# Two-layer binary convolution and local attention: new priorities and costs in a list planner, and the first image's channel sums on VectorE

## The chip, the cores and the metric

The kernel runs on one core of a Trainium2 chip. The metric is device time in microseconds (us) of one launch. The engines are TensorE (PE in the profile; PEld are its weight loads), VectorE (DVE), ScalarE (ACT), GpSimd (POOL) and SyncE (SP), which here only issues DMAs.

## The reference, cut to what matters

The input x has 16 images of 256 channels, 56 x 56 pixels, float32. Two layers follow each other, each a residual addition of a function of the group-normalized input (`_gn`: 32 groups of 8 channels).

```python
# layer 0
xq = sign(_gn(x) + bias)
for i, d in enumerate((1, 3, 5)):            # dilations
    wq = scale_i * sign(w[i] - mean(w[i]))   # binary weights, forward value
    y = conv3x3(xq, wq, dilation=d, groups=4) + cb[i] - move1[i]
    y = where(y >= 0, y, alpha[i] * y) + move2[i]
    out = out + y
out = (out - mean(out, channels)) * rsqrt(var(out, channels) + eps)
x = x + out * gamma + beta
# layer 1
q, k, v = split(_gn(x) @ qkv_w.T + qkv_b)     # 8 heads of 8 channels
k, v = branch(k) + rpb, branch(v)             # 9 neighbours, plus a learned 3x3 depthwise conv
attn = softmax over the 9 neighbours of sum_c(q * k)
x = x + (sum_9(attn * v) @ proj_w.T + proj_b)
```

The 3 x 3 neighbourhood of a pixel is the window of keys and values for that pixel.

## The kernel before, in words

An image is cut by halves of its rows: 128 partitions hold 64 channels of one group (there are NG = 4 groups g) for two half images. For the later steps a half is cut again into strips of 7 rows, so that one *unit* u (of NU = 2) covers 128 x 784 elements per group.

Per image b the steps are these, each with the name of its stage in the table `ORDER`:

- `signs`: loads the four groups as `xh` (three buffers), takes their sum and their sum of squares with two ACT passes (`stats`, L424: Identity and Square with an accumulated output), turns them into a shift per channel (`norm0`, lines L382 to L443) and writes the sign as bfloat16 into `sgn[g]` (stage "sign", L449), with two small DMAs for the rows at the border of the halves (`halo`). The first image has its own stage "start" that does all of it group by group from one load; later images load every group twice.
- `conv` ("conv0", "conv1" for the two units): per group and dilation 36 matmuls (L499) into one PSUM tile `ps` of two banks (there are four), then ACT and DVE steps (L518, L525, L531, L537) that add the parametric ReLU into `ct` (seven buffers). For one tile that is one ACT and two DVE steps, or two and one for the first dilation.
- `channel_norm` ("mean", "var", "root", "scale" for each unit): sums over channels by matmul (L548, L566), the normalized result, and its addition to `xt` (three buffers, loaded from x in stage "load") on POOL (L638) with a square pass on ACT (L645).
- `fold` and `qkv`: group norm of the second layer is folded into the weights (L667 to L717); six groups of 32 matmuls (L729) and ACT evictions (L747) fill `qt`, `kt`, `vt`, of which there is one each.
- `scores` ("prod", "term", "soft"): nine products q * shifted k (L785, POOL), ten groups of matmuls over heads (L807), then a softmax with DVE transposes (L821 to L843).
- `attend` ("value", "proj"): ten groups of matmuls (L857), products with shifted v (L869, DVE), sums of these (L883, POOL), projection (L903), the last addition (L914) and the store.

Nothing of the order of these operations is written out by hand. The code that builds the kernel first collects every operation in a `Plan`, with engine, an assumed cost, what it reads and writes, which buffers it takes, and a priority: twice the image number plus a number from `ORDER` for its stage and index (lower goes first). `Plan.emit` then simulates all engines at build time: among the operations that are ready and have their buffers, each engine's candidate is the one that can start first; an operation of better priority is preferred if it starts at most `AHEAD` later. The engine whose candidate starts first emits it. Buffers of the kinds xh, xt, ct, p and m are handed out in the order of their creation. A result is seen by another engine `HOP` later. `either` marks operations that POOL or DVE may do; DVE is a candidate only if it would end more than `LEAN` before POOL (for the last image `LAST`, a negative number). A set `port` flag keeps such an operation apart from POOL's in the plan. On the chip the engines then run their queues in that order and wait on semaphores for what they read and write.

Three lines carry the rule:

```python
self.prio = 2 * b + ORDER[stage][i]
elif start + cost + o.lean > done: continue
if e not in best or start < best[e][0] - self.AHEAD: best[e] = (start, x, e, cost)
```

Of the kernel before, what the change touches and what calls it, by code (L numbers as in the profile page):

```python
# [68 lines left out]
class Op:  # L69
# [6 lines left out]

ORDER = {
    "first": (-3.81,),
    "second": (88.59,),
    "start": (-2.38, 18.89, -7.71, 3.29),  # L80
    "weights": (-4.65, -9.01, 0.64, 24.68, 23.33, 21),
    "stats": (10.49, 30.86, 22.58, 94.91),
    "norm0": (32.82,),
    "sign": (19.48, 99.46, -6.27, -5.4),
    "conv0": (-1.69, 4.96, 26.11, 0.66, 0.85, 19.36, -4.07, -1.86, 4.93, -11.22, -8.26, 19.59),
    "conv1": (-5.78, -8.78, 98.87, 0.22, 0.26, 6.89, -8.83, 30.63, 33.62, 1.84, 19.38, 25.39),
    "load0": (90.92,),
    "load1": (8.24,),
    "mean0": (-9.77,),
    "mean1": (20.13,),  # L90
    "var0": (-12.01, -8.88, 19.47, -0.22),
    "var1": (-14.66, 26.56, 89.22, -12.67),
    "root0": (23.78,),
    "root1": (-9.89,),
    "scale0": (100.7, 21.53, 3.58, 99.01),
    "scale1": (-10.73, -4.27, -0.4, 21.4),
    "fold": (-8.77,),
    "qkv0": (-0.15, -11.55, 19.01),
    "qkv1": (10.85, 1.84, 96.23),
    "prod0": (28.81, -0.84, -7.11, -6.13, -10.3, 7.62, -0.09, -4.95, 20.71),  # L100
    "prod1": (27.44, 23.38, -3.2, 99.25, 31.01, -10.92, -1.88, -1.61, -3.25),
    "term0": (19.37, 27.66, 25.15, 17.81, -9.38, 9.45, -1.68, 20.87, -1.36, 21.48),
    "term1": (24.14, 22.52, 28.6, 3.33, 8.91, 2.55, 1.92, 35.5, 4.7, 21.73),
    "soft0": (-4.91,),
    "soft1": (7.25,),
    "value0": (8.34, -0.46, -5.88, 1.95, 0.4, 8.91, 0.58, 26.08, -5.98, 34.72),
    "value1": (21.66, 7.27, 7.39, -4.86, -1.41, 9.39, 20.85, -1.49, -3.81, 90.17),
    "proj0": (0.69, 1.29, 9.01, -2.1),
    "proj1": (-14.76, 0.33, -4.01, -0.55),
# [3 lines left out]
class Plan:  # L113
# [7 lines left out]
    HOP = 0.1  # L121
    LEAN = 26.94
    LAST = -11.31
    AHEAD = 0.13

    def __init__(self, kinds):
        self.kinds, self.ops, self.wrote, self.read = kinds, [], {}, {}
        self.prio = 0.0
        self.queues = {k: [] for k in ("xh", "xt", "ct", "p", "m")}
# [106 lines left out]
def preact_conv_attention(  # L236
# [107 lines left out]
    def act(cost, f, r, w):  # L344
        op("ACT", 0.94 * cost, f, r, w)
# [887 lines left out]
```

## Time and profile before

| | |
|---|---|
| median of 3 runs | 2155.05 us (2154.48 to 2155.28) |
| the profiled execution's own time | 2157.43 us |
| its span, first to last instruction | 2154.9 us |
| mean granted TensorE clock | 0.948 |
| instructions | 70853 |
| DMA: read / written HBM | 154.91 MB / 51.38 MB, 96 GB/s over the span |

Busy time is the share of the span in which an engine has an instruction under way. Idle time is put down to what ended it, as far as semaphores show that. The chain of waits is followed backward from the last instruction: to what released each step, or to the step before it on its engine. Matmuls are pipelined, and their ends are modelled, so a busy PE isn't PE at its peak. "issue" is idle time for which the profile shows no releaser.

### The profile page before, as it was taken

How to read it: one execution, taken by the hardware profiler on the slowest of the kernel's cores; microseconds unless marked ns; L12 is line 12 of the kernel's file. 1: busy time of each engine (PE TensorE's matmuls, PEld its weight loads, DVE VectorE, ACT ScalarE, POOL GpSimd, SP SyncE). 2: the span in 40 equal slices, each digit the busy share in tenths (PEclk: the TensorE clock that was granted, in tenths of full speed). 3: DMA queues.
4: the chain of work that ended last, by engine and by line, in shares of the span. 5: the costliest groups of instructions: out<-in, count | busy, mean ns of one | idle time of the engine just before them, and what ended most of it. 6: DMA issues, size and time to landing. Idle time of an engine off the chain costs nothing.

```text
span 2154.9 us, 70853 instructions
## 1 busy us (share of the span) xinstructions
PE 1823.2 (85%) x31770; PEld 889.5 (41%) x31770; DVE 1697.7 (79%) x2327; ACT 1189.6 (55%) x1581; POOL 1276.5 (59%) x762
## 2 busy tenths in 40 slices
PE   6679898888989889898988989898898989879684
PEld 5444353434435343443534344353434435434231
DVE  7676969789696977969698796968879696986856
ACT  8675556565565756556575655647565565533220
POOL 2116657585675748557574865747486574746743
PEclk9889999999999999999999999999999999989896
DMA  8742534644453454445445444644444454041212
GB/s 208 165 92 67 123 79 111 130 95 91 110 130 83 111 121 97 93 104 133 91 111 117 100 94 95 138 94 111 108 102 101 95 133 100 7 100 23 61 31 60
DMA packets 102416, 216.26 MB, mean 100 GB/s; under 512 B 10720, under 2 KB 84832, under 8 KB 102112
## 3 DMA queue, kind: packets, MB, share of 16 engines
q1 hardware_dynamic: 102112, 211.74, 44.5%
q8 instruction: 248, 4.06, 0.8%
q14 instruction: 56, 0.46, 0.1%
HBM read 154.91 MB, written 51.38 MB: 96 GB/s over the span
## 4 chain that ended last, share of the span: by engine, by line
PE 42%; DVE 32%; POOL 10%; ACT 7%; issue 7%; DMA 2%; SPq 0%; POOLq 0%; DVEq 0%; ACTq 0%
PE banks L499 13%; PE banks L729 10%; PE banks L807 8%; POOL m L883 6%; DVE m L869 6%; DVE ct L537 6%; PE banks L857 5%; DVE ct L525 5%; DVE xt L914 4%; ACT banks L531 3%; DVE ct L595 3%; POOL xt L638 2%; PE banks L566 2%; PE banks L903 2%; DVE et L821 1%
## 5 line engine op out<-in xcount | busy, mean ns | idle before, releaser
L499 PE MATMUL banks<-sgn,wconv 64*64 64x392 bf16 x13824 | 680.2, 340 | 78.9 <-DVE m L869 32.1
L785 POOL TENSOR_TENSOR p<-qt,kt 128x784 f32<-128x784 f32 x276 | 467.0, 1726 | 326.2 <-ACT kt L762 179.3
L883 POOL TENSOR_TENSOR m<-m 128x784 f32<-128x784 f32 x251 | 478.3, 1906 | 248.1 <-DVE m L869 232.8
L499 PEld LDWEIGHTS <-wconv 64*64 64x64 bf16 x13824 | 438.6, 107 | 373.4 <-issue 217.4
L531 ACT ACTIVATE banks<-banks,cbi,csc 128x784 f32<-128x784 f32 x384 | 370.2, 973 | 203.2 <-DVE ct L525 192.4
L537 DVE SCALAR_TENSOR_TENSOR ct<-banks,oalpha,ct 128x784 f32<-128x784 f32 x384 | 389.4, 1027 | 98.4 <-ACT banks L531 89.3
L525 DVE SCALAR_TENSOR_TENSOR ct<-banks,asc,ct 128x784 f32<-128x784 f32 x256 | 262.0, 1024 | 186.9 <-PE banks L499 180.7
L857 PE MATMUL banks<-at,wv 64*32 64x392 f32 x5120 | 300.0, 533 | 61.3 <-DVE m L869 44.2
L638 POOL TENSOR_TENSOR xt<-xt,ct 128x784 f32<-128x784 f32 x128 | 237.2, 1860 | 190.4 <-DVE ct L624 189.6
L869 DVE TENSOR_TENSOR m<-banks,vt 128x784 f32<-128x784 f32 x288 | 278.2, 969 | 54.8 <-PE banks L857 48.7
L807 PE MATMUL banks<-p,wk 32*64 32x392 f32 x4608 | 245.4, 517 | 38.6 <-POOL p L785 38.2
L729 PE MATMUL banks<-xt,wf 64*64 64x392 f32 x3072 | 269.0, 496 | 2.8 <-POOL wf L667 2.8
L424 ACT ACTIVATE junk<-xh 128x1568 bf16<-128x1568 f32 x128 | 193.2, 1509 | 103.2 <-DMA xh<-in_x 101.4
L645 ACT ACTIVATE junk<-xt,pr 128x784 bf16<-128x784 f32 x128 | 121.2, 947 | 106.4 <-POOL xt L638 105.2
L602 ACT ACTIVATE sq<-ct 128x784 f32<-128x784 f32 x128 | 109.4, 857 | 125.2 <-DVE ct L595 102.5
L518 ACT ACTIVATE ct<-banks,asc 128x784 f32<-128x784 f32 x128 | 116.4, 910 | 98.8 <-PE banks L499 87.5
L729 PEld LDWEIGHTS banks<-xt,wf 64*64 64x64 f32 x3072 | 116.0, 134 | 129.2 <-issue 104.4
L857 PEld LDWEIGHTS banks<-at,wv 64*32 64x32 f32 x5120 | 63.3, 108 | 220.6 <-DVE m L869 110.9
L807 PEld LDWEIGHTS banks<-p,wk 32*64 32x64 f32 x4608 | 80.3, 133 | 161.1 <-POOL p L785 83.0
L903 PE MATMUL banks<-m,wp 64*64 64x392 f32 x1024 | 122.3, 584 | 26.1 <-DVE m L891 21.8
L595 DVE SCALAR_TENSOR_TENSOR ct<-ct,mv,banks 128x784 f32<-128x784 f32 x128 | 125.4, 1023 | 17.4 <-PE banks L566 17.4
L914 DVE SCALAR_TENSOR_TENSOR xt<-banks,prb,xt 128x784 f32<-128x784 f32 x128 | 128.1, 1028 | 10.4 <-PE banks L903 9.7
(102 smaller groups left out, 1518.8 us busy)
## 6 DMA issues: line engine op xcount, KB each, us to landing
xh<-in_x SPq DMA_DIRECT2D x248, 392.0 KB, 5.6
xt<-in_x SPq DMA_DIRECT2D x128, 392.0 KB, 7.1
out<-xt SPq DMA_DIRECT2D x128, 392.0 KB, 5.8
sgn<-sgn SPq DMA_DIRECT2D x128, 41.2 KB, 4.7
p<-in_w SPq DMA_DIRECT2D x12, 144.0 KB, 5.9
wq<-in_wqkv SPq DMA_DIRECT2D x1, 384.0 KB, 6.1
cst<-in_consts SPq DMA_DIRECT2D x1, 336.0 KB, 2.9
wk<-in_wk_a SPq DMA_DIRECT2D x1, 320.0 KB, 5.8
```

The source lines that it names most:

```text
L499: nc.tensor.matmul(out=ps[q * GC : (q + 1) * GC, h, 0:SN], lhsT=wconv[h * GC : (h + 1) * GC, g, d, tap, :], rhs=sgn[g][h * GC : (h + 1) * ...
L525: lambda: nc.vector.scalar_tensor_tensor(ct.tile, n(), asc[:, g, s], ct.tile, ALU.mult, ALU.add),
L531: lambda: nc.scalar.activation(n(), n(), AF.Relu, bias=cbi[:, g, s], scale=csc[:, g, s]),
L537: lambda: nc.vector.scalar_tensor_tensor(ct.tile, n(), oalpha[:, g, s], ct.tile, ALU.mult, ALU.add),
L638: lambda e, g=g: e.tensor_tensor(xt[:, g], xt[:, g], ct[g].tile, ALU.add),
L729: nc.tensor.matmul(out=ps[h * D : (h + 1) * D, q, 0:SN], lhsT=wf[q * GC : (q + 1) * GC, g, j, :], rhs=xt[q * GC : (q + 1) * GC, g, h, :], ...
L785: e.tensor_tensor(p.tile.rearrange("p x (r w) -> p x r w", w=W), _view(qt[:, 0, u * SN :], [(NU * SN + LANES, 2), (W, SR), (1, W)]), shift ...
L807: nc.tensor.matmul(out=ps[rt // 2][q * 64 : (q + 1) * 64, rt % 2, 0:n], lhsT=wk[r, j, :], rhs=rhs, start=s == 0, stop=s == 9,)
L857: nc.tensor.matmul(out=ps[rt * 32 : (rt + 1) * 32, q, 0:SN], lhsT=wv[q * 64 : (q + 1) * 64, j, :], rhs=at[q * 64 : (q + 1) * 64, rt, 0:SN] ...
L869: lambda j=j, m=m, ps=ps: nc.vector.tensor_tensor(m.tile.rearrange("p x (r w) -> p x r w", w=W), _view(ps[:, 0, :], [(512, 2), (W, SR), (1 ...
L883: lambda e, m=m, acc=acc: e.tensor_tensor(acc.tile, acc.tile, m.tile, ALU.add),
L914: lambda g=g, ps=ps: nc.vector.scalar_tensor_tensor(xt[:, g], ps[:, :, 0:SN], prb[:, g : g + 1], xt[:, g], ALU.add, ALU.add),
```

## The change

Every number in `ORDER` is replaced, as are the four constants of the plan. The table gets keys of their own for the first image (`^`) and the last (`$`); in this version their numbers equal those of the images between. Nearly all assumed costs are lowered, and the common factors 0.94 (ACT) and 0.965 (DVE) go. The first image's four Identity passes on ACT become four `tensor_reduce` on DVE; the Square passes stay. The diff, cut; of the three spellings of a new key the plain one is shown:

```diff
 ORDER = {
-    "first": (-3.81,),
-    "second": (88.59,),
-    "start": (-2.38, 18.89, -7.71, 3.29),
-    "weights": (-4.65, -9.01, 0.64, 24.68, 23.33, 21),
-    "stats": (10.49, 30.86, 22.58, 94.91),
-    "norm0": (32.82,),
-    "sign": (19.48, 99.46, -6.27, -5.4),
-    "conv0": (-1.69, 4.96, 26.11, 0.66, 0.85, 19.36, -4.07, -1.86, 4.93, -11.22, -8.26, 19.59),
-    "conv1": (-5.78, -8.78, 98.87, 0.22, 0.26, 6.89, -8.83, 30.63, 33.62, 1.84, 19.38, 25.39),
-    "load0": (90.92,),
-    "load1": (8.24,),
-    "mean0": (-9.77,),
-    "mean1": (20.13,),
-    "var0": (-12.01, -8.88, 19.47, -0.22),
-    "var1": (-14.66, 26.56, 89.22, -12.67),
-    "root0": (23.78,),
-    "root1": (-9.89,),
-    "scale0": (100.7, 21.53, 3.58, 99.01),
-    "scale1": (-10.73, -4.27, -0.4, 21.4),
-    "fold": (-8.77,),
-    "qkv0": (-0.15, -11.55, 19.01),
-    "qkv1": (10.85, 1.84, 96.23),
-    "prod0": (28.81, -0.84, -7.11, -6.13, -10.3, 7.62, -0.09, -4.95, 20.71),
-    "prod1": (27.44, 23.38, -3.2, 99.25, 31.01, -10.92, -1.88, -1.61, -3.25),
-    "term0": (19.37, 27.66, 25.15, 17.81, -9.38, 9.45, -1.68, 20.87, -1.36, 21.48),
-    "term1": (24.14, 22.52, 28.6, 3.33, 8.91, 2.55, 1.92, 35.5, 4.7, 21.73),
-    "soft0": (-4.91,),
-    "soft1": (7.25,),
-    "value0": (8.34, -0.46, -5.88, 1.95, 0.4, 8.91, 0.58, 26.08, -5.98, 34.72),
-    "value1": (21.66, 7.27, 7.39, -4.86, -1.41, 9.39, 20.85, -1.49, -3.81, 90.17),
-    "proj0": (0.69, 1.29, 9.01, -2.1),
-    "proj1": (-14.76, 0.33, -4.01, -0.55),
+    "first^": (24.59,),
+    "second^": (30.61,),
+    "start^": (-0.44, 12.01, 8.32, -11.9),
+    "weights^": (16.57, 0.74, 15.54, 8.13, -15.35, 9.81),
+    "stats": (-23.02, -11.03, 24.25, 43.57),
+    "norm0": (-20.32,),
+    "sign": (-8.81, 4.11, 13.27, 36.85),
+    "conv0": (-17.27, 2.29, 28.55, -15.99, 8.45, 8.78, -5.4, 6.78, 31.53, -11.69, 14.22, 14.25),
+    "conv1": (7.4, 12.95, 95.96, 12.79, 1.59, 12.9, 4.7, 39.18, 55.69, -8.93, 9.19, 30.54),
+    "load0": (95.98,),
+    "load1": (5.24,),
+    "mean0": (8.83,),
+    "mean1": (29.44,),
+    "var0": (8.78, 11.01, 15.97, 29.02),
+    "var1": (-9.01, 16.63, 18.58, 16.63),
+    "root0": (-10.53,),
+    "root1": (-17.05,),
+    "scale0": (15.67, 15.06, -3, 40.43),
+    "scale1": (-16.84, 17.23, 8.22, 8.83),
+    "fold": (-12.89,),
+    "qkv0": (6.66, -12.93, 15),
+    "qkv1": (8.11, -17.4, 96.15),
+    "prod0": (9.09, 30.51, 9.14, -13.48, 29.6, 14.43, 17.51, -16.64, -13.31),
+    "prod1": (-14.1, 12.39, 13.44, 5.73, 7.96, 13.89, -14.32, -16.31, -9.81),
+    "term0": (-17.28, 5.04, -6.13, -15.6, 8.43, 19.29, 31.53, 24.74, -8.75, 0.82),
+    "term1": (-16.84, 29.94, 29.34, 11.93, 6.96, 8.07, -9.43, 13.66, 9.05, 6.97),
+    "soft0": (-14.93,),
+    "soft1": (7.31,),
+    "value0": (-13.35, -23.05, -1.34, 4.34, -6.07, 9.15, -16.95, -21.09, -15.61, 39.19),
+    "value1": (-19.04, 4.84, -9.61, -12.73, 6.92, 7.45, 12.47, 8.08, 28.72, 39.07),
+    "proj0": (-0.81, 7.32, -11.88, -8.96),
+    "proj1": (15.51, -16.48, -1.88, 6.47),
 }
...
-    HOP = 0.1
-    LEAN = 26.94
-    LAST = -11.31
-    AHEAD = 0.13
+    HOP = 0.25
+    LEAN = 61.83
+    LAST = -32.05
+    AHEAD = 0.29
...
     def at(self, stage, b, i=0):
+        stage += "^" if b == 0 else "$" if b == self.last else ""
...
     def act(cost, f, r, w):
-        op("ACT", 0.94 * cost, f, r, w)
+        op("ACT", cost, f, r, w)
...
     def dve(cost, f, r, w, two=False):
-        op("DVE", 0.965 * cost, f, r, w, port=two)
+        op("DVE", cost, f, r, w, port=two)
...
-    def stats(g, xh, sums):
+    def stats(b, g, xh, sums):
         for func, col, key in ((AF.Identity, g, "sums"), (AF.Square, NG + g, "squares")):
+            if b == 0 and key == "sums":
+                dve(
+                    1.7,
+                    lambda: nc.vector.tensor_reduce(sums[:, g : g + 1], xh.tile, AX.X, ALU.add),
+                    [xh],
+                    [(sums, key)],
+                    True,
+                )
+                continue
             act(
-                1.72,
+                1.56,
...
-        pe(1.75, products, [("sgn", g), ("halo", g), ("wconv", g, d)], [ps], [ct])
+        pe(1.65, products, [("sgn", g), ("halo", g), ("wconv", g, d)], [ps], [ct])
...
             dve(
-                1.03,
+                0.945,
                 lambda: nc.vector.scalar_tensor_tensor(ct.tile, n(), asc[:, g, s], ct.tile, ALU.mult, ALU.add),
...
-            either((1.87, 0.97), product, deps, [p], b)
+            either((1.7, 0.9), product, deps, [p], b)
...
-            pe(0.9, f, [at, "attention"], [ps], [m] if m else [])
+            pe(0.83, f, [at, "attention"], [ps], [m] if m else [])
```

## The prediction

> **What bounds the kernel now.** I read the page first, then busy time in windows, then the chain of waits, then the timelines of single engines. No engine is full over the span (the page's table of engines):
>
> ```profile
> PE 1823.2 (85%) x31770; PEld 889.5 (41%) x31770; DVE 1697.7 (79%) x2327; ACT 1189.6 (55%) x1581; POOL 1276.5 (59%) x762
> ```
>
> The first multiplication of a "qkv" stage marks where an image's attention begins: at 157.2 us for the first image, then every 126.2 us (920.3 and 1046.5, for instance), then at 1939.1 for the fifteenth and 2056.0 for the sixteenth. Cut there, the busy time in windows shows a start, a periodic middle and an end (columns: length, busy time and instruction count of PE, weight load, DVE, ACT, POOL, then granted clock, DMA share, GB/s):
>
> ```profile
> 0.00:157.20 157.20, 106.40 (x1858) 72.00 (x1862) 112.50 (x236) 120.47 (x156) 29.73 (x23) 0.86 0.71 159
> 157.20:1939.10 1781.90, 1565.33 (x27630) 759.01 (x27622) 1441.31 (x1924) 1024.19 (x1358) 1130.42 (x672) 0.97 0.46 102
> 1939.10:2154.90 215.80, 151.45 (x2294) 58.52 (x2292) 143.85 (x168) 44.93 (x68) 116.34 (x67) 0.86 0.20 44
> ```
>
> PE is idle for 157.2 - 106.4 = 50.8 us of the start, 216.6 of the middle and 64.3 of the end: 331.7 in all. One period in slices shows what an order can still win:
>
> ```profile
> 920.30:935.30 15.00, 15.00 (x191) 7.92 (x192) 6.80 (x9) 8.79 (x11) 3.93 (x3) 1.00 0.84 177
> 935.30:950.30 15.00, 14.84 (x292) 6.47 (x284) 6.95 (x7) 5.09 (x7) 10.97 (x7) 1.00 0.23 52
> ...
> 980.30:995.30 15.00, 10.38 (x216) 5.20 (x209) 14.74 (x16) 12.62 (x17) 13.70 (x8) 1.00 0.62 141
> 995.30:1010.30 15.00, 14.30 (x272) 7.16 (x271) 14.41 (x16) 8.87 (x15) 4.42 (x4) 1.00 0.22 48
> 1010.30:1025.30 15.00, 11.78 (x226) 5.10 (x218) 14.54 (x17) 7.07 (x9) 11.80 (x7) 1.00 0.84 185
> ```
>
> In the first 30 us PE is full and DVE under half busy; from 980 on DVE is full and PE waits. So a period of 126.2 us is PE-bound first and DVE-bound later, with 111.1 us of PE work and 102.8 of DVE work. Who waits for whom, in the same period, says at which operations: columns are the waiting line, the releaser, total us, times, longest.
>
> ```profile
> PE banks L857 <- DVE m L869: 2.5, 5, 1.2
> PE banks L807 <- POOL p L785: 2.5, 1, 2.5
> PE banks L499 <- DVE m L869: 2.4, 2, 1.2
> PE banks L548 <- ACT sq L602: 2.2, 2, 1.7
> PE banks L566 <- DVE lv L617: 2.1, 1, 2.1
> ```
>
> These are the value stage (L857, L869), the score terms (L807), the variance (L548) and the spread of the root (L566): no single wait is large. The whole-span chain of waits agrees, and bears on every part of the change:
>
> ```profile
> PE 42%; DVE 32%; POOL 10%; ACT 7%; issue 7%; DMA 2%; SPq 0%; POOLq 0%; DVEq 0%; ACTq 0%
> ```
>
> [...] 744 ns for 576 elements (L1005), 1117 for 936 (L840), 1.036 ns an element. [...]
>
> **The change part by part.** The sum is made on the profiled execution: its own time is 2157.4 us for a span of 2154.9; the median of the runs is 2155.05, 2.4 lower.
>
> *First image's sums.* ACT loses four Identity passes of 1.63 us (one starts at 10.71, the next pass at 12.34), 6.5 in all. DVE gains four reduces; from the two rows above, 744 + 992 x 1.036 = 1772 ns each, 7.1 in all. Between 0 and 45 us ACT carries much of the chain: the first group's sum and square passes end at 13.95, its sign waits until 19.11, its convolution until 24.45. The third and fourth groups' passes are in the chain at 20.66 and 30.94 to 34.06. Sum and square now run side by side. I count three of four passes as won: 3 x 1.63 = -4.9, taken as -5. The DVE reduces are covered, since DVE is busy 112.5 of 157.2 us; uncovered they cost 7.1. Ends: -6.5 and +3. Queued behind a reduce on DVE are the weights' sums (L1003 to L1005) and the small norm steps, and for these the signs wait.
>
> *Start loads.* The key of "start" (-0.44 for group 0) now precedes all keys of "weights" (16.57 for the first pair, before -4.65), and "second" goes from 88.59 to 30.61. On SP the image halves may so be issued ahead of weights: 12 issues of 144 KB, some 0.6 us each, 5.9 us to land. Then 1 MB of attention weights comes earlier among the halo copies. In the trace the first sign's halo is issued at 20.79 and the convolution starts at 24.45, so a weight pair landing 3 us later still fits. Taken as 0; ends -3 and +4.
>
> *New costs, HOP, AHEAD.* They add no instruction. The old costs were 5 to 6% above the trace's distances (a conv 1.75 against 1.65: three in a row take 4.95; a DVE step 0.965 x 1.03 = 0.994 against 0.945). HOP goes the other way: DVE to ACT starts 1.07 us after a start (943.27 to 944.34), so 0.125 over the distance, DVE to POOL 1.11 against 0.885 (978.12 to 979.23), 0.225: 0.25 is at the upper edge. Throughput is now counted right and latency a little too long. They act only through the order.
>
> *LEAN, LAST.* With 26.94 as with 61.83 DVE takes an operation from POOL only far behind it. The trace has 12 products (L785) and 5 sums (L883) on DVE, out of the last image's 18 and 16. LAST -32.05 widens an offer that was already open. Taken as 0; ends -3 and +3, a product costing 0.97 on DVE and 1.73 on POOL.
>
> *New keys.* Averages over a stage show a direction. A lower key goes first. Attention comes forward: "term0" from 12.9 to 4.2, "term1" 15.4 to 9.0, "value0" 6.8 to -4.5, "value1" 14.5 to 6.6, "prod1" 17.8 to -0.1, "soft0" -4.9 to -14.9, "fold" -8.8 to -12.9. The convolution that fills goes back ("conv1" 16.1 to 22.8; "conv0" 4.1 to 5.4). Next image's statistics and signs come forward ("stats" 39.7 to 8.4, "norm0" 32.8 to -20.3, "sign" 26.8 to 11.4), "scale0" from 56 to 17. A key counts for two per image, so 8 points outweigh four images: these are real reversals wherever both are ready. Each moved step takes its DMAs with it: sixteen half loads (392 KB, 5.6 us), eight halo copies, eight xt loads and eight stores an image, all in SP's one order; on POOL, whose order is one too, a product (1.73 us) put ahead of a sum holds that sum and with it the value stage's three m tiles. For each stage taken first, the work that hides its latency is the convolution behind it. If earlier attention feeds DVE during the first 30 us, where it idles 16 of 30, PE waits less later. Bounds: nothing, or all 15.1 us of PE idle per period, or a loss. I take a tenth, 1.5 us, in 13 periods: -19.5. The tenth is a choice: it is what one saved gap from the list of waits is worth, less something given back. After the saved wait the next late thing is POOL (80.8 of 126.2 busy): its sums hold the value stage.
>
> *End.* It has its own stalls: 5.0 us before the projection at 2015.7, then store, xt load (8.0), four POOL additions (7.3) up to 2056. The keys of first and last image equal the common ones. Taken as 0; ends -12 and +8.
>
> Sum: -5 - 19.5 = -24.5; 2157.4 - 24.5 - 2.4 = 2130.5, so **2130 us**.
>
> **Rivals.** *Slower: second-unit convolutions come late.* "conv1" has keys 95.96, 39.18 and 55.69, and lies behind attention. Unit 1's normalization needs the last of it, the fold both units, and the next qkv the fold. From its first sum (1008.2) to the next qkv (1046.5) the trace takes 38 us; of work it holds about 25: sums, spread and variance 8, root and spread 4, scale and four POOL additions (1.9 each) 9, square and fold 4. Other PE work covers it now. If 3 us of it stay bare per period, 13 x 3 = 39, less 5 at the start: 2155 + 34 = 2189. It decides once more than 5/13 = 0.4 us stay bare net of any gain. For it: the second half of the period has DVE full. Against it: fold and qkv (-17.4 for k) are urgent and next image's "conv0" can fill.
>
> *Large gain.* A third of the middle's PE idle goes: 216.6/3 = 72, with the start's 5: 2078. For it: DVE's empty first 30 us. Against it: POOL and four PSUM tiles still throttle the value stage.
>
> *No difference.* The order changes only what waits where and the start's gain is absorbed before the first qkv: 2150 to 2159. For it: no single wait is over 2.5 us of a period.
>
> *The change doesn't do what it says:* the reduces run, but the first convolution waits for weights now issued later. Then the start's -5 is 0 and the rest stands: 2135, inside the likeliest case.
>
> **How the numbers follow.** 0.2% (4.3 us) is about what a measurement tells from no change. Modest gain, 2090 to 2150: 0.37. Large gain below 2090: 0.14. Within 0.2%: 0.05. Slower: 0.44; a new list order can open stalls as easily as close them. So faster 0.51, same 0.05, slower 0.44. The predicted time is the modest gain's. The range reaches into both signs: 2075 leaves about 0.1 below, 2208 (4 us bare per period: 2155 + 52) about 0.1 above.
>
> **What would show it.** Right: four tensor reduces over 1568 elements on DVE of about 1.77 us, ACT's passes on xh 124 instead of 128; first convolution by 22 us; first qkv by 152; a period near 124.7 with DVE busier in its first 30 us; 17 or so shared operations on DVE at the end. Wrong: a period over 126.2 with PE waiting on L617, L602 or the fold; PE clock in the middle under 0.97; a first convolution waiting for weight loads.

## The result and the profile after

The changed kernel takes 2147.62 us (median of 20 runs, 2142.92 to 2155.07); the kernel before, run beside it, 2156.13. The ratio is 0.9964, with a 95% interval of 0.9956 to 0.9973: faster by 8.5 us, a third of the 25 us forecast. The profiled execution has a span of 2150.0 us, 4.9 less than before; single executions of the changed kernel differ by up to 12 us, so profile and median needn't give the same difference.

The page's table of engines of the changed kernel:

```profile
PE 1794.7 (83%) x31770; PEld 885.7 (41%) x31770; DVE 1711.5 (80%) x2336; ACT 1187.0 (55%) x1573; POOL 1270.2 (59%) x757
```

PE is busy 28.5 us less with the same number of matmuls, while the span shrinks by only 4.9: PE is idle for longer (355.3 us against 331.7). Cut at the first qkv of the first and of the fifteenth image, as before (same columns):

```profile
0.00:159.80 159.80, 106.90 (x1963) 72.26 (x1967) 121.77 (x243) 119.42 (x153) 29.82 (x23) 0.90 0.70 157
159.80:1931.10 1771.30, 1536.28 (x27560) 753.80 (x27553) 1441.13 (x1922) 1022.78 (x1354) 1132.05 (x672) 0.97 0.46 102
1931.10:2150.00 218.90, 151.48 (x2262) 59.64 (x2257) 148.63 (x173) 44.83 (x67) 108.34 (x62) 0.85 0.21 45
```

The start is 2.6 us longer by these rounded cuts (2.8 by the exact first qkv, 157.03 and 159.79), the middle 10.6 shorter, the end 3.1 longer. The middle falls apart once more. Times between the first qkv of one image and of the next:

| period | before | after | difference |
|---|---|---|---|
| second image's (1st) | 131.6 | 127.0 | -4.6 |
| the next, 12 of them, mean | 126.31 | 126.50 | +2.3 in all |
| the one up to the fifteenth image | 134.6 | 126.3 | -8.3 |
| the last | 117.0 | 118.8 | +1.8 |
| last qkv to the end | 98.9 | 100.2 | +1.3 |

With the start's +2.8 these make the -4.9 (rounding aside). The twelve periods in which the new order was to win have won nothing; two periods at the two ends have. Of these the -8.3 is the firm one: the kernel before with only its sums changed has 134.7 there, and three runs with the new keys and all of the work have 124.0 to 126.3. Start and second image's period together give -1.8: the second image's qkv is at 286.8 in place of 288.6. Two other runs with the new list and no more work have it at 284.9 (two v buffers) and 289.3 (less POOL work), so this is not told from scatter.

One such period in slices:

```profile
918.50:933.50 15.00, 14.79 (x174) 7.15 (x172) 6.76 (x9) 7.37 (x10) 3.11 (x2) 1.00 0.80 167
933.50:948.50 15.00, 14.00 (x296) 6.48 (x292) 7.90 (x8) 5.15 (x7) 13.17 (x9) 1.00 0.01 2
...
978.50:993.50 15.00, 10.67 (x178) 4.98 (x171) 13.42 (x15) 12.05 (x15) 13.65 (x9) 0.89 0.66 155
993.50:1008.50 15.00, 14.24 (x288) 7.56 (x287) 14.67 (x26) 8.99 (x17) 6.67 (x4) 1.00 0.50 105
1008.50:1023.50 15.00, 12.85 (x260) 5.82 (x252) 14.99 (x17) 7.43 (x12) 9.41 (x6) 1.00 0.80 172
```

DVE does 14.66 us in the first 30 (13.75 before): its half-empty first 30 us are nearly as empty as they were. Over the whole of this period PE is busy 109.5 of 126.65 us, idle 17.1 (before 15.1). What PE waits for in it:

```profile
PE banks L872 <- POOL p L850: 4.2, 4, 2.4
PE banks L564 <- DVE m L934: 2.4, 2, 1.2
PE banks L631 <- DVE lv L682: 1.9, 1, 1.9
PE banks L922 <- DVE m L934: 1.6, 3, 1.2
PE banks L922 <- DVE at L908: 1.5, 1, 1.5
```

L872 is the score term, L564 the convolution, L631 the spread, L922 the value (L807, L499, L566, L857 before). The chain that ended last has shifted a little from PE (42% before) to DVE (32%):

```profile
PE 39%; DVE 37%; POOL 7%; issue 6%; DMA 5%; ACT 5%; SPq 2%; DVEq 0%; POOLq 0%; ACTq 0%
```

One period is a small sample; the same view over ten of them (420 to 1680 us) shows where the gain went. The kernel before:

```profile
PE banks L857 <- DVE m L869: 26.6, 50, 1.2
PE banks L807 <- POOL p L785: 25.0, 10, 2.5
...
PE banks L566 <- DVE lv L617: 21.1, 10, 2.1
PE banks L548 <- ACT sq L602: 20.2, 17, 1.7
PE banks L566 <- DVE ct L537: 8.8, 20, 0.7
```

The changed kernel:

```profile
PE banks L872 <- POOL p L850: 41.8, 40, 2.5
...
PE banks L922 <- DVE m L934: 15.7, 30, 1.2
PE banks L922 <- DVE at L908: 14.9, 10, 1.6
PE banks L968 <- DVE m L956: 11.9, 20, 0.8
...
PE banks L564 <- DVE xt L979: 11.0, 18, 0.6
PE banks L613 <- ACT sq L667: 9.3, 10, 0.9
```

The waits for squares (20.2 to 9.3 us), for value products (26.6 to 15.7) and for the normalized `ct` in the spread (8.8, now none) shrink. The convolution's own wait for value products (L934) stays, at 24.7 before and 24.0 after. In place of the others stand longer waits for POOL's products q * k (25.0 to 41.8), for the softmax (L908, 14.9), for the sum ahead of the projection (L956, 11.9) and for the last addition (L979, 11.0). In all, PE is idle for 168.6 of these 1260 us, where it was for 151.5 before. Attention was brought forward, and its operands are now what PE waits for.

Where the period before the fifteenth image lost 8.3 us is also visible. Windows from the fourteenth to the fifteenth first qkv, the kernel before:

```profile
1804.50:1939.10 134.60, 114.58 (x1970) 53.29 (x1971) 102.82 (x127) 61.14 (x81) 80.06 (x48) 0.92 0.30 67
```

and the changed one:

```profile
1804.80:1931.10 126.30, 110.28 (x1974) 53.72 (x1971) 101.67 (x128) 60.00 (x80) 80.87 (x48) 0.96 0.29 62
```

The same work is done; before, the first value group of unit 1 began 90.1 us after its image's qkv, where the twelve periods ahead of it have 75.5 to 77.5. It stood behind a late softmax (POOL's L842 waited 11.1 us for DVE's L841), and the granted clock fell to 0.92. In the changed kernel it begins after 73.5 us, and POOL's wait is 0.2 us.

### The profile page after: what moved, and what is told of

The parts are those of the page before. It is cut to its first block, busy times and chain, and to the rows that moved or that the text cites. A ratio compares the mean times of both kernels' runs of the same rounds, so it can differ in the third digit from the quotient of the medians.

```text
span 2150.0 us, 70814 instructions
## 1 busy us (share of the span) xinstructions
PE 1794.7 (83%) x31770; PEld 885.7 (41%) x31770; DVE 1711.5 (80%) x2336; ACT 1187.0 (55%) x1573; POOL 1270.2 (59%) x757
## 4 chain that ended last, share of the span: by engine, by line
PE 39%; DVE 37%; POOL 7%; issue 6%; DMA 5%; ACT 5%; SPq 2%; DVEq 0%; POOLq 0%; ACTq 0%
PE banks L794 11%; PE banks L872 10%; DVE m L934 10%; PE banks L564 9%; DVE ct L602 8%; POOL p L850 5%; DVE ct L590 5%; PE banks L922 3%; DMA out<-xt 3%; DVE xt L979 3%; PE banks L613 2%; ACT banks L596 2%; DVE ct L660 2%; PE banks L968 1%; DVE at L908 1%
## 5 line engine op out<-in xcount | busy, mean ns | idle before, releaser
L564 PE MATMUL banks<-sgn,wconv 64*64 64x392 bf16 x13824 | 683.6, 343 | 86.5 <-DVE m L934 37.3
L564 PEld LDWEIGHTS <-wconv 64*64 64x64 bf16 x13824 | 433.9, 108 | 377.2 <-issue 195.6
L922 PE MATMUL banks<-at,wv 64*32 64x392 f32 x5120 | 289.7, 529 | 60.6 <-DVE at L908 31.5
L934 DVE TENSOR_TENSOR m<-banks,vt 128x784 f32<-128x784 f32 x288 | 276.0, 966 | 44.2 <-PE banks L922 42.6
L872 PE MATMUL banks<-p,wk 32*64 32x392 f32 x4608 | 247.2, 518 | 67.3 <-POOL p L850 67.0
L489 ACT ACTIVATE junk<-xh 128x1568 bf16<-128x1568 f32 x124 | 186.9, 1507 | 100.9 <-DMA xh<-in_x 99.5
L794 PEld LDWEIGHTS banks<-xt,wf 64*64 64x64 f32 x3072 | 113.3, 134 | 141.1 <-issue 123.1
L872 PEld LDWEIGHTS banks<-p,wk 32*64 32x64 f32 x4608 | 82.8, 133 | 197.6 <-POOL p L850 135.9
L922 PEld LDWEIGHTS banks<-at,wv 64*32 64x32 f32 x5120 | 67.9, 110 | 223.0 <-issue 117.1
L514 ACT ACTIVATE sgn<-xh,g 128x1568 bf16<-128x1568 f32 x64 | 105.7, 1651 | 69.9 <-PE banks L564 67.9
L660 DVE SCALAR_TENSOR_TENSOR ct<-ct,mv,banks 128x784 f32<-128x784 f32 x128 | 124.5, 1024 | 23.3 <-PE banks L631 23.3
L968 PE MATMUL banks<-m,wp 64*64 64x392 f32 x1024 | 114.8, 551 | 28.5 <-DVE m L956 28.5
L979 DVE SCALAR_TENSOR_TENSOR xt<-banks,prb,xt 128x784 f32<-128x784 f32 x128 | 128.1, 1027 | 8.4 <-PE banks L968 7.7
```

Source lines behind the costliest of these rows:

```text
L564: nc.tensor.matmul(out=ps[q * GC : (q + 1) * GC, h, 0:SN], lhsT=wconv[h * GC : (h + 1) * GC, g, d, tap, :], rhs=sgn[g][h * GC : (h + 1) * ...
L794: nc.tensor.matmul(out=ps[h * D : (h + 1) * D, q, 0:SN], lhsT=wf[q * GC : (q + 1) * GC, g, j, :], rhs=xt[q * GC : (q + 1) * GC, g, h, :], ...
L872: nc.tensor.matmul(out=ps[rt // 2][q * 64 : (q + 1) * 64, rt % 2, 0:n], lhsT=wk[r, j, :], rhs=rhs, start=s == 0, stop=s == 9,)
L922: nc.tensor.matmul(out=ps[rt * 32 : (rt + 1) * 32, q, 0:SN], lhsT=wv[q * 64 : (q + 1) * 64, j, :], rhs=at[q * 64 : (q + 1) * 64, rt, 0:SN] ...
L934: lambda j=j, m=m, ps=ps: nc.vector.tensor_tensor(m.tile.rearrange("p x (r w) -> p x r w", w=W), _view(ps[:, 0, :], [(512, 2), (W, SR), (1 ...
L979: lambda g=g, ps=ps: nc.vector.scalar_tensor_tensor(xt[:, g], ps[:, :, 0:SN], prb[:, g : g + 1], xt[:, g], ALU.add, ALU.add),
```

## The experiments

All ratios are to the kernel before, run on the same chip. The middle is told by the time from qkv to qkv, in the one profiled execution of each run. In five of these executions, marked *, PE's first instruction comes at 11.40 us in place of 5.75 or 5.76: 5.6 us of their first qkv belong to that start and not to the edit. What is left still scatters by a microsecond or two among runs with the changed kernel's list.

| run | us | ratio [95%] | first qkv | periods in the middle |
|---|---|---|---|---|
| the changed kernel | 2147.62 | 0.9964 [0.9956, 0.9973] | 159.8 | 126.3 to 126.8 mostly |
| sums alone | 2161.67 | 1.002 [1.0012, 1.0029] | 167.2 | 128.6 once, then 126.1 to 126.9, 128.9 once |
| changed, sums on ACT | 2169.9 | 1.0057 [1.0041, 1.0073] | 162.4 | 148.0 once, then 124.3, 126.3 |
| changed, start's keys old | 2185.38 | 1.0126 [1.0109, 1.0143] | 174.0 | 147.6 once, then 127.3, 126.3 |
| new costs, old keys | 2339.51 | 1.0846 [1.0825, 1.0866] | 173.7* | 136.1 to 147.2 |
| new keys, old costs | 2482.91 | 1.1503 [1.1473, 1.1532] | 172.2 | 134 to 158 |
| DVE 4.3 us less | 2141.19 | 0.9923 [0.9906, 0.994] | 160.7 | 126.3 |
| PE 4.4 us less | 2143.8 | 0.9944 [0.9933, 0.9955] | 159.7 | 126.1 to 127.2, 128.4 once |
| POOL 3.7 us less | 2150.37 | 0.9966 [0.9954, 0.9978] | 165.5* | 123.8 once, 126.3 to 127.8 |
| two v buffers | 2148.41 | 0.996 [0.9947, 0.9973] | 161.0 | 123.9 once, then 125.2 to 127.6 |
| DVE 3.8 us less, unit 1 | 2143.73 | 0.992 [0.9905, 0.9935] | 165.5* | 123.1 and 123.2, then 126.1 to 126.6 |
| DVE 3.8 us less, unit 0 | 2148.52 | 0.9948 [0.9933, 0.9963] | 158.0 | 123.9 once, then 126.3, later 125.2 to 127.9 |
| PE 4.1 us less, in the qkv | 2097.62 | 0.9709 [0.9694, 0.9723] | 160.5 | 120.5 to 125.7, mean 123.3 |
| PE 1.4 us more | 2163.2 | 1.0029 [1.0015, 1.0043] | 159.2 | 129.0, 127.6, 125.8 in turn |
| PE 2.7 us more | 2190.65 | 1.0154 [1.0104, 1.0205] | 164.4* | 129.7 |
| PE 1.4 us less | 2127.85 | 0.9863 [0.9844, 0.9883] | 160.3 | 123.0 or 126.2, some 125 |
| four savings at once | 2093.94 | 0.9718 [0.9697, 0.9738] | 159.7 | 120.5 to 125.6, mean 122.8 |
| gaps filled at the terms | 2145.64 | 0.994 [0.9923, 0.9957] | 160.7 | 125.7 to 127.6, mean 126.3 |
| the same, and matmuls added at the values | 2165.02 | 1.0028 [1.0018, 1.0039] | 165.3* | 127.0 to 128.5, mean 127.7 |

### The parts of the change

In the expectations, A is the theory that the new keys of the start make the start late, B that the reduces do.

**Sums alone.** The kernel before, with nothing changed but the sums (the edit cut, the call on one line):

```diff
+            if b == 0 and key == "sums":
+                dve(1.7, lambda: nc.vector.tensor_reduce(sums[:, g : g + 1], xh.tile, AX.X, ALU.add), [xh], [(sums, key)], True)
+                continue
```

> The kernel before, with the first image's four channel sums moved to VectorE and nothing else (old keys, costs, constants). Theory A: the sums shorten the start, and what the full change lost there came from the new load order. First sign near 15 to 17 us instead of 19.1, first qkv 2 to 5 us before 157.0, total 0.997 to 0.999 of before. Theory B: the reduces on VectorE hold the weight preparation queued behind them. First convolution not before 24.4, first qkv at 157 or later, total 1.000 or more.

A reduce takes 1.785 us, as forecast (1.77). Yet the first qkv comes at 167.2 in place of 157.0 and the fourth sign at 53.77 in place of 39.54: in the old order the fourth reduce stands on DVE behind other work until 35.45, and PE takes its result (L382) only at 48.13, after convolutions that stand ahead of it in PE's order; before it did so at 36.01. The first convolution comes at 29.48 (before 24.45). So B's three numbers came true in this order. Ten microseconds are lost at the first qkv, where -5 was forecast. The profiled execution is the longest of the run's 22 and keeps all of them (its span is 10.4 us longer); by the median the run loses 4.8.

**Sums back on ACT in the changed kernel.**

```diff
-            if b == 0 and key == "sums":
+            if False:
```

> The changed kernel with the four sums back on ScalarE. Theory A: the first qkv comes 1 to 5 us later than the changed kernel's 159.8, total some 0.998 to 0.999 of before. Theory B: VectorE is freed for the weights, first convolution earlier than 33.3 and the first qkv at or before 158, total 0.994 to 0.996.

It is slower by 22 us (2169.9 against 2147.6; 20 by the two ratios). In the profiled executions 2.6 of this are at the first qkv, and 21 in one period, the second image's, of 148.0. So the value of the sums on DVE depends on the rest of the list: +5 in one order, -22 in the other. The build-time simulation starts from other times, and the list falls out differently: by the traces each engine's order differs from the changed kernel's up to the third image's qkv and is the same from there on.

**The old keys of the start in the changed kernel** ("first", "second", "start", "weights"; two of the four shown).

```diff
-    "start^": (-0.44, 12.01, 8.32, -11.9),
-    "weights^": (16.57, 0.74, 15.54, 8.13, -15.35, 9.81),
+    "start^": (-2.38, 18.89, -7.71, 3.29),
+    "weights^": (-4.65, -9.01, 0.64, 24.68, 23.33, 21),
```

> The changed kernel with the old keys of the four stages that only the first image has: first, second, start, weights. Theory A: weights are loaded ahead of the second and third image half again, first convolution by 22 us instead of 33.3, first qkv at 150 to 156 instead of 159.8, total 0.992 to 0.995 of before. Theory B: first convolution still past 28 and the first qkv within 2 us of 159.8. Periods after the second stay near 126.4 under both.

In the changed kernel SP issues all three image buffers first and the weights after them; timeline of SP, changed kernel (start, length, queue, line, transfer, count):

```profile
1.64 3.83 SPq L468 DMA_DIRECT2D xh<-in_x  x6
5.52 6.80 SPq L1060 DMA_DIRECT2D p<-in_w  x6
```

and before:

```profile
1.64 2.50 SPq L995 DMA_DIRECT2D p<-in_w  x4
4.19 1.24 SPq L412 DMA_DIRECT2D xh<-in_x  x2
```

So the first sign comes at 14.86 (before 19.11), but the first weights' sign only at 18.22 (7.52), and the first convolution at 33.35 (24.45). With the old keys it comes at 24.95 as before. And still the first qkv is 14 us later than in the changed kernel, since soon after, PE waits for a halo copy:

```profile
46.08 0.54 PE L564 MATMUL banks<-sgn,wconv 64*64 64x392 bf16 x3
55.98 4.33 PE L564 MATMUL banks<-sgn,wconv 64*64 64x392 bf16 x52 [9.37 <-DMA sgn<-sgn]
```

It stood in SP's order behind four loads of `xt` (issued from 41.58 on), was issued at 48.99 and landed at 55.94. The late first convolution is real, but the queue behind it decides: A falls as a statement on the first qkv, and so does B, which had it within 2 us of 159.8. The second image's period, 147.6, adds another 20.6.

**Costs without keys, keys without costs.** The first run takes the changed kernel with the table of before; the second the kernel before with the new table and the reduces.

> The changed kernel (new costs, new constants, sums on VectorE) with all keys of before. Theory K: the keys make the changed kernel's end: the fifteenth period goes back from 126.4 to 131 to 136 us and the total is 0.998 to 1.003 of before. Theory C: the costs make it: fifteenth period near 126 and the total 0.995 to 0.997. The middle periods stay between 125.5 and 128 if the order matters little there (theory D: VectorE-bound second part of the period); a new order far off, 129 or more, speaks against D.

> The kernel before with the new keys and the sums on VectorE, but the old costs and the old four constants. If keys and costs are one unit (the old keys on the new costs gave 1.085 of before): 1.01 to 1.09 of before, with middle periods of 128 to 140. If the new keys are good in themselves: 0.995 to 1.003 with periods near 126.

They are 8.5% and 15.0% slower than the kernel before, where the first was expected at 0.995 to 1.003 and the second, if the two belong together, at 1.01 to 1.09: both are further off. Keys and costs are one unit: a table belongs to the costs with which the simulation turns it into a list. The changed kernel's small gain is thus no sum of parts.

### What holds the middle at 126.3 us

Four runs take the changed kernel's list as it is and shorten one engine, or give one buffer more:

```diff
-        dve(1.04, lambda: nc.vector.tensor_reduce(mx.tile, ev(), AX.X, ALU.max), [et], [mx])
-        dve(1.13, lambda: nc.vector.tensor_tensor(ev(), ev(), wide(mx), ALU.subtract), [mx], [et], True)
+        dve(1.04, lambda: None, [et], [mx])
+        dve(1.13, lambda: None, [mx], [et], True)
```

> The changed kernel in the same order, leaving out two VectorE instructions per unit: the softmax's row maximum (1.04 us) and its subtraction (1.13 us), 4.3 us per image; the softmax is the same in exact arithmetic. Theory D (the second part of each period is bound by VectorE, whatever the order): middle periods fall from 126.4 by 3 to 4.3 us, total 0.970 to 0.978 of before. Theory P (TensorE's work of 109.5 us and its gaps bind): by 1 or less, total 0.988 or more. Theory L (a latency chain through all engines, where each step counts only while it is in the chain): by 1.5 to 3.

```diff
-            for tap in range(9):
+            for tap in range(8):
...
-                        stop=tap == 8,
+                        stop=tap == 7,
```

> The changed kernel in the same order, leaving out the ninth tap of every convolution: 4 of 36 matmuls, 0.18 us each, 4.4 us of TensorE per image. Its output differs by that tap. Theory D: middle periods fall by 0 to 2 us (only the convolutions in the TensorE-bound first 45 us count). Theory P: by 3 to 4.4. Theory L: by 1 to 2.5.

```diff
-                        lambda e, m=m, acc=acc: e.tensor_tensor(acc.tile, acc.tile, m.tile, ALU.add),
+                        lambda e, m=m, acc=acc, j=j: None if j == 4 else e.tensor_tensor(acc.tile, acc.tile, m.tile, ALU.add),
```

> The changed kernel in the same order, leaving out one of the eight sums per unit in the value stage (1.85 us on GpSimd, 3.7 per image). Its output lacks the fifth of the nine neighbours. Theory D and P: middle periods fall by 0 to 1 us. If GpSimd's sums hold the value stage, as the prediction had it: by 2 to 3.7.

```diff
-    QKV = (1, 1, 1)
+    QKV = (1, 1, 2)
```

> The changed kernel with two buffers for v instead of one, so that the next image's v needn't wait for the last product of this one; the order is reckoned anew from the same keys. Theory B (the single buffers keep the qkv and score phase apart from the value phase, and so VectorE idle for 15 of the first 30 us): VectorE busier there, middle periods 121 to 125. If v alone isn't what separates the phases (k and q, or the PSUM tiles): within 1.5 us of 126.4, or longer, since the keys were not chosen for it.

None of them moves the period: 126.3 with 4.3 us of DVE gone, 126.1 to 127.2 (128.4 once) with 4.4 of PE gone. What they gain lies in single periods at either end. So D (DVE binds) falls by the first run, P (PE binds) by the second, L (a chain through all engines) by both, and by the third POOL's sums don't hold the value stage. The fourth is a weak test, since the list that the planner made with two buffers is the same as with one. The first of them, which leaves out only the shift by the maximum, a factor that cancels in the softmax, is at 0.9923 ahead of both kernels. Next, whether it is the stretch in which DVE is full (theory Z): the subtraction of the mean (L660) is left out in unit 1, which lies there, then in unit 0, which doesn't.

```diff
-                lambda g=g: nc.vector.scalar_tensor_tensor(
+                lambda g=g: None if u == 1 else nc.vector.scalar_tensor_tensor(
```

> The changed kernel in the same order, leaving out the four subtractions of the channel mean of unit 1 (L660; the output is not centred there): 4 x 0.945 = 3.8 us of VectorE per image, between 1013 and 1020 in the period that starts at 918.5. Theory Z (the period is a row of zones, each with its own bound: TensorE alone for the first 54 us, VectorE alone for the last 50): middle periods fall from 126.4 by 2.5 to 3.8. Theory F (a fixed pace outside the four engines, which three different savings of some 4 us left at 126.3): by less than 0.5.

> The twin of the run before: the same four subtractions left out for unit 0, the same 3.8 us of VectorE per image, but between 944 and 949, where TensorE is full. Theory Z: middle periods fall by 0 to 0.5 us. Theory F: the same. A fall of 2 us or more speaks against both.

With unit 1's steps gone two periods take 123.1 and 123.2, and then the list is back at 126.1 to 126.6, where Z had 122.6 to 123.9 throughout. Z falls. The fourth group of channels left out of every qkv product was the first edit that moved the middle:

```diff
-            for g in range(NG):
+            for g in range(NG - 1):
```

> The changed kernel in the same order, leaving out the fourth channel group of the qkv products: 8 of 32 matmuls in each of six groups, 6 x 0.68 = 4.1 us of TensorE per image, all in the first 36 us of the period. Theory Z: middle periods fall by 3 to 4.1 us, where the ninth tap's 4.4 us, spread over the period, gave 0.2. Theory F: by less than 0.5.

The periods swing between 120.5 and 125.7, by 123.3 in the mean, the size that Z had for this run. That 4.1 us of PE give 3 here, and 4.4 give nothing in the convolution, led to theory W: that the periods favour whole steps of the granted clock. The traces show the step: the clock records of the changed kernel (88) and of the kernel before (92) hold only full and half clock, and change only on a grid of 3.413 us. Thirty-seven such steps are 126.29 us, 36 are 122.88, 38 are 129.71. The changed kernel, columns as before, in stretches of about a step:

```profile
956.20:959.60 3.40, 2.75 (x64) 1.10 (x56) 3.01 (x6) 1.82 (x2) 3.40 (x2) 1.00 0.49 96
959.60:963.00 3.40, 0.92 (x16) 0.24 (x16) 3.29 (x4) 2.37 (x4) 3.40 (x4) 1.00 0.00 0
963.00:966.40 3.40, 3.36 (x40) 0.99 (x48) 1.61 (x4) 0.00 (x0) 3.40 (x3) 0.50 0.89 201
...
980.10:983.50 3.40, 1.43 (x32) 0.29 (x17) 3.22 (x4) 2.34 (x4) 3.06 (x3) 1.00 0.56 133
983.50:986.90 3.40, 2.96 (x36) 1.80 (x35) 2.27 (x3) 1.82 (x3) 3.32 (x3) 0.50 0.81 202
```

In the second row PE waits for POOL's products (2.43 us), in the fourth for DVE's value products (1.21); the row after each runs at half clock, and a group of convolution matmuls takes 3.12 us there and 1.74 elsewhere. Between 420 and 1680 us, 21 steps run at half clock, in 20 stretches (one of two steps). The 3.41 us ahead of each stretch hold 0.92 to 1.62 us of PE work, and of the steps that full clock follows only one holds less than 1.64 (1.49). From one image to the next the half-clock steps like the third row begin 126.29 us apart (457.83, 584.12, 710.41, 836.71, 963.00). Since all changes of the clock in this trace lie on the grid, any two stretches lie whole steps apart, so this alone shows nothing; the periods themselves are the evidence, as with unit 1's subtractions left out, where nine of them in a row take 126.22 to 126.30.

If periods favour whole steps, they must not answer to small changes of PE's work in proportion. These three runs issue the first group of some qkv products twice (the first result is overwritten), or leave the last out (the first run's edit, cut):

```diff
-            for g in range(NG):
+            for g, z in [(0, True)] * (u == 0 and j < 2) + [(g, g == NG - 1) for g in range(NG)]:
```

> The changed kernel in the same order, with two of an image's six qkv groups computing their first quarter twice: 2 x 0.68 = 1.4 us more TensorE work per image in the TensorE-full part of the period, same output. Theory W [...]: nearly all middle periods at 126.3 or at 129.7 us, none settled at 127.7. Theory L (the cost passes through): 127.7.

> The same with four of the six groups: 2.7 us more TensorE work per image. Theory W: middle periods at 129.7 (or still 126.3). Theory L: 129.0.

> The changed kernel in the same order, with two of the six qkv groups leaving out their last quarter (q and k of unit 0 lack the fourth channel group): 1.4 us less TensorE work per image. Theory W: middle periods at 126.3 or at 122.9. Theory L: 125.0.

With 2.7 us more, thirteen periods are 129.7 to a tenth. PE's timeline of that run, the first qkv matmuls of three images:

```profile
683.23 6.77 PE L794 MATMUL banks<-xt,wf 64*64 64x392 f32 x80
...
812.93 6.75 PE L794 MATMUL banks<-xt,wf 64*64 64x392 f32 x80
...
942.63 6.75 PE L794 MATMUL banks<-xt,wf 64*64 64x392 f32 x80
```

They are 129.70 and 129.70 apart: 38 steps, 0.7 more than the added work. This is one execution of two. The other took 2181.54 us in place of 2199.75, at a mean clock of 0.958 in place of 0.936; even if 5.6 of the 18.2 us between them are the late start, its periods can't all have been 129.7 unless start and end gave the rest; by an estimate that spreads it over the thirteen, they were 128.3 to 128.7 in the mean, near the linear 129.0. With 1.4 us less, periods are mostly 123.0 or 126.2 to 126.5, 36 or 37 steps, and seldom the 125 of a linear answer, though the twelve in the middle are 125.1 in the mean. With 1.4 more, three periods take turns (129.0, 127.6, 125.8) and close after 382.4 us, 112 steps (382.3); in the mean that is 1.2 more, near a linear answer. The run with new costs and old keys, far slower, has nine of its periods at 136.5 to 136.6 or 139.9 to 140.3, where 40 and 41 steps are 136.5 and 139.9. So periods of whole steps occur in single executions, but not strictly.

The four savings (DVE twice, PE in the convolution, POOL) in one kernel:

> The changed kernel in the same order with four savings together that alone left the middle periods at 126.3: the softmax's shift by its maximum, the ninth tap of the convolutions, unit 1's subtraction of the channel mean, and one of eight sums per unit on GpSimd; 8.1 us of VectorE, 4.4 of TensorE and 3.7 of GpSimd per image. Theory W: [...] middle periods at 122.9 or 119.5, total 0.955 to 0.975 of before. Theory F (a fixed pace that only the qkv products touch): 126.3 again, 0.985 to 0.993.

One by one they left the middle where it was; together they make 2093.94 us, with a mean period of 122.8. That is close to one step less, but the periods scatter from 120.5 to 125.6 and keep to no whole steps. A plainer reading fits as well: where the engines take turns as the last thing waited for, a saving on one leaves the others, and savings on all three pass through. This run doesn't tell the two apart.

**Is the half clock the cause?** The last two runs were to fill the idle PE time ahead of the half-clock stretches with small matmuls into columns of a PSUM tile that nothing reads. Their expectations take theory W further: the half clock makes the period. The second adds the line below in every value group; its table gives six matmuls each to the seventh to ninth group of unit 0 (the edits cut):

```diff
+                fill(("term", b, u), {(1, 6): 14, (1, 7): 4}, u, ps[0])
...
+                fill(("value", b, u), {(0, 7): 6, (0, 8): 6, (0, 9): 6}, u, ps, True)
```

> The changed kernel in the same order, with extra TensorE work where it waits 2.43 and 0.74 us for POOL's products (sixth and seventh score term of unit 1): 14 and 4 small matmuls into columns of the PSUM tile that nothing reads; about 2.9 us of idle time filled per image. In the changed kernel TensorE is busy 0.92 us of the 3.4 before the half-clock stretch at 963.0. If [...] (Theory W): no half-clock stretch follows the score terms any more, and either the period falls below 126 us or another stretch, at the value stage, keeps it at 126.3; total 2120 to 2152. If the half clock only accompanies a period that DVE sets: the stretch goes and the period stays at 126.3 everywhere. If the extra work itself is late: periods over 127, total over 2160.

> As the run before, and six small matmuls of some 1 us in all behind each of the seventh, eighth and ninth value groups of unit 0, where TensorE waits 1.2 us for a PSUM tile. If [...] (Theory W): hardly a half-clock stretch is left in the middle, its granted clock is over 0.985 (0.97 in the changed kernel), and the period is no longer held at 126.3 but falls to 122.5 to 125.5; total 2095 to 2140. If DVE sets the period: clock over 0.985 as well, but periods of 126.3 and a total of 2145 to 2155. If the extra matmuls delay the DVE products that read the same tiles: periods over 127.

With the terms' gap filled, the stretch behind it goes, but others come: 19 half-clock steps in the same 1260 us. Periods scatter from 125.7 to 127.6, and their mean is 126.3 with 3 us more of PE work each. So one gap closed does not free the period; what this run gains in total (0.994) lies in single periods at either end (124.1, 125.0, 115.5). The second run does not do what was meant. PE and DVE in it, at one value group of unit 0:

```profile
988.59 1.18 PE L845 MATMUL banks<-cst 128*32 128x96 f32 x12
989.87 0.97 DVE L942 TENSOR_TENSOR m<-banks,vt 128x784 f32<-128x784 f32 x1 [0.49 <-PE banks L845]
990.90 1.74 PE L564 MATMUL banks<-sgn,wconv 64*64 64x392 bf16 x36 [1.14 <-DVE m L942]
```

The added matmuls (L845) write the tile that the product on DVE reads, and are part of its group: the product waits for them, and PE then still waits 1.14 us for the product, where it waited 1.20 without them. Three such sets per image put 3.5 us more into this chain. Some 12 half-clock steps are left. Ten periods, changed kernel:

```profile
420.00:1680.00 1260.00, 1091.37 (x19644) 535.32 (x19642) 1027.29 (x1377) 739.54 (x979) 808.63 (x480) 0.97 0.48 106
```

matmuls added at both places:

```profile
420.00:1680.00 1260.00, 1131.63 (x20122) 581.18 (x20114) 1022.51 (x1352) 729.61 (x962) 800.73 (x476) 0.98 0.48 106
```

one tap left out of the convolution:

```profile
420.00:1680.00 1260.00, 1074.23 (x18656) 509.53 (x18658) 1030.40 (x1375) 736.77 (x977) 808.21 (x480) 0.95 0.48 106
```

The clock rose to 0.98, not over 0.985, and the period did not fall to 122.5 to 125.5: it rose to 127.7. That is what was expected for matmuls that delay the products, so this run neither upholds theory W nor refutes it, and whether the half clock makes the period stays open. The last row shows a saving swallowed, though. One tap less is 4.4 us of PE per image at full clock, but PE's busy time falls by 1.7 per period (17.1 in ten), with the clock at 0.95 in place of 0.97: of 44 us in ten periods, 27 are still there. Half-clock steps go from 21 to 34. PE is busy nearly throughout them (110.6 us in the 34, 66.4 in the 21), and half of the 44.2 us between, 22, is what the lower clock costs, by this estimate, of the 27; the other 5 are not accounted for. PE is idle for 185.8 us of these 1260 without the tap, for 168.6 with it. That the added half-clock steps follow steps of little PE work, as the 20 stretches above do, is an inference.

## Why the prediction was right or wrong

*Direction and size.* Faster came true, but by luck: neither of the two terms that made the forecast faster holds, and the gain came from a stall that the working did not have. 2130 was off by 17.6 us, and 2147.62 lies in the range. The failing step is the middle: **"I take a tenth, 1.5 us, in 13 periods: -19.5"**. Its twelve like periods measured +0.2 us each, +2.3 in all. Two things failed in it. A saved wait was taken for a saved microsecond: the ten-period waits show old ones gone and others in their place, and idle PE time went from 15.1 to 17.1 us in the period shown. And the answer was taken as linear: savings of 3.7 to 4.4 us on each of three engines left the period at 126 to 127. Why they did is open in part. The idea of filling DVE's empty first 30 us gave 0.9 us of DVE work there.

*First image's sums, -5.* The price of a reduce was right (1.785 against 1.77). The use of it was wrong: "three of four passes as won" took ACT for the end of the chain, but alone in the old order the reduces cost 10 us at the first qkv (in the new one, taking them back costs 2.6 there). The step named what queues behind them (weights' sums, norm steps), and did not price it. The signs of "right" it gave, a first convolution by 22 us and a first qkv by 152, measured 33.35 and 159.8.

*Start loads, 0.* Wrong. The weights behind three image buffers put the first convolution at 33.35, +8.9, where "landing 3 us later still fits". This is the rival *the change doesn't do what it says*, which named the waiting first convolution; at the first qkv only 2.8 of it was left, and the second image's period gave 4.6 back. Start and second period together are -1.8, where -5 was forecast; even the -1.8 is not told from scatter.

*Costs, LEAN, LAST at 0.* Not to be judged alone: new costs with old keys are 1.0846, new keys with old costs 1.1503. The working treated the costs as neutral and the keys as the change; the two are one. At the end 22 shared operations were on DVE (14 products, 8 sums), 17 before: little, as said.

*End, 0 (-12 to +8).* From the fifteenth qkv on, where the prediction cut, it measured 1.8 + 1.3 = +3.1, and with the period before it -5.2, both inside the ends given. That period's -8.3 is nearly all of the gain. The working's own times show the stall: 14 periods of 126.2 from 157.2 end at 1924.0, and the fifteenth qkv is at 1939.1. The 15.1 us between lie in two odd periods (131.6 and 134.6), and both lost their excess.

*The clock.* A clock under 0.97 in the middle was to be one of the signs of "wrong". It was 0.97 in the ten periods both times, and no wait of PE in them was longer than 2.5 us, before or after; half-clock steps stand in them all the same, 20 before and 21 after.

*Rivals.* Second-unit convolutions late: no period grew by 3 us. Large gain: no. No difference (2150 to 2159): the median is 2.4 us under it, and its mechanism, "the order changes only what waits where", is what the middle shows.

## What to carry to other kernels

A sum of waits is no forecast of a period: ask what is late next, and try the size of the answer by taking a few microseconds of work out of one engine in the same list. In a list that a build-time simulation makes, keys and assumed costs are one object, and an edit to one image can move another. Read the times of one mark in every image before you speak of a period: the odd ones can hold the gain. Before crediting a saving on PE, look in the trace for half-clock stretches behind those of little PE work: here, with 4.4 us less of PE per image, there were 34 half-clock steps in place of 21. And look in the trace whether added work fell into the gap it was meant for.

## What the runs showed of the hardware

Between 420 and 1680 us of the changed kernel, all 20 half-clock stretches follow 3.41 us in which PE was busy 0.92 to 1.62 us, and no single wait of PE was over 2.5 us. The clock records change on a grid of 3.413 us, before and after. Single executions have periods near whole steps of it: 126.3 (DVE less), 129.7 (2.7 us more), 136.5 and 139.9 (old keys), against 126.29, 129.71, 136.5 and 139.9 for 37, 38, 40 and 41 steps. Others don't: 125.1 in the mean with 1.4 us less, and 128.3 to 128.7 by estimate in the second execution with 2.7 us more. Three single savings (4.3 us of DVE, 4.4 of PE in the convolutions, 3.7 of POOL) left most middle periods at 126.1 to 127.8, 4.1 us of PE in the qkv took them to 123.3 in the mean, and four savings together to 122.8 (2093.94 us, part of the work left out). What ties the period to the steps is argued, not shown: filling one of two gaps ahead of half-clock stretches left the mean at 126.3, and the run that was to fill both delayed the products instead (127.7).
